# Remainders of the experts' rows in blocks of two 64-row halves, each half with its own expert's weights

## The chip, the cores and the metric

The kernel runs on one core of a Trainium2 chip. A core has five engines with queues of their own: TensorE (PE, matrix products; its weight loads are listed as PEld), VectorE (DVE), ScalarE (ACT), GpSimd (POOL) and SyncE (SP), which here does nothing but start transfers. DMA engines move data between the chip's memory and the on-chip buffers. The engines run side by side and wait for each other by semaphores; each takes its own instructions in the order in which the program lists them. The metric is the device time of one execution in microseconds (us), as the median of several runs.

## The reference

One layer of a transformer on `x` of 4 x 1024 rows by 512, in float32. The rows are normalized, then attention with 16 heads (causal mask, a bias that falls with distance) and a mixture of experts are both computed from the normalized rows, and all is added:

```
xn = layernorm(x)
out = x + attention(xn, Wq, bq, Wk, bk, Wv, bv, Wo, bo) + experts(xn, gate_w, w1, w2)

# experts: T = 4096 rows, E = 8 experts, TOP_K = 2, I = 352
probs = softmax(x @ gate_w.T)
topw, sel = top_k(probs, 2);  topw = topw / sum(topw)
g, u = split(x @ w1[e].T)                  # 512 -> 2 x 352
expert_out[e] = (silu(g) * u) @ w2[e].T    # 352 -> 512
out = sum over the two selected e of topw * expert_out[e]
```

Each row goes to two of the eight experts, so there are 8192 pairs of row and expert. How many fall to each expert is known only when the kernel runs.

## The kernel before, in words

**Routing.** After the normalization, `route()` (L479) works out on VectorE where each pair goes. The pairs are sorted by expert into blocks of 128 rows, and each expert's last block is filled up with empty rows. Eight experts can leave eight partly filled blocks, so the program has `NBLK` = 71 blocks (L76) whatever the data: (8192 - 8) // 128 + 8. `blocks` is the number of blocks of each expert, `ends` its running sum, `slot` the place of each pair, `eid` (L523) the expert of each block, and `token` (L585) the row that stands in each place. The table of `token` is made by matmuls (L539, `fill_table`) from 0/1 matrices `col`, `place` and `both`, which VectorE and ScalarE prepare. Pieces of the attention's projections (`pq`, `pk`, `pv`) are placed by hand between these steps on TensorE (L1268 to L1275).

**A block** (`expert_pieces`, L675) is computed in pieces:
- `gate(k)` (L737): first `turn_act(k - 1)` (L756), which transposes the activations of the block before (`pact`) and copies them out as `actT`, by VectorE and ScalarE; then four matmuls of 128 x 128 by 352 columns into `pgate` (L728), then tanh on ScalarE and a product on VectorE.
- `up(k)` (L748): four such matmuls into `pup`, a product on VectorE, then `load_w1(k + 1)`, then `turn(k + 1)`, which transposes the next block's rows (`pxs`, L721).
- `second_layer(k)` (L795): `down(k - 1)` (L770), three matmuls of up to 128 x 128 by 512 columns into `ye` (L776), an addition on VectorE (L785), the write of the block to `ys_d` (L786, on SyncE), `load_w2(k)`; then `load_rows(k + 3)`, a gather on GpSimd's queue.

A float32 matmul stands in the profile as two records, a transpose as one. So a block's gate is eight records, its second layer six.

**Weights.** All weights are read again for every block, because the block's expert is known only at run time: SyncE reads the expert's number from `eid` into a register (`value_load`, L681) and issues the loads with it. `w1` comes in four tiles of 352 KB (128 of the 512 input rows, gate and up together), in a ring of six buffers; `w2` in three tiles of 256, 256 and 192 KB, in a ring of four. A load into a buffer waits until the matmuls that read its former content are done. SyncE also issues the writes of `ys_d` and `o_d` and the other loads, all in program order: a transfer that waits holds those behind it.

**The order of the work.** Attention runs over 16 units (4 batches x 4 groups of four heads), in 12 steps each: `scores` (`s`), `values` (`o`), and for the next unit `largest` (`m`, the row maxima). All other pieces (the experts' pieces, the projections, the output rows) are in lists, each with a weight in us. `fill` (L1187) pops them one by one between the attention's steps, at an even rate; so the order on every engine is fixed when the program is built. The experts' pieces begin before the first unit's scores. The output rows follow the last block: `y` is the output projection, added to the two gathered expert rows.

The matmuls of `values` (L1084) use the array in strips: each of four heads has 128 x 32 weights and writes 32 partitions of the same `o`.

Of the kernel before, what the change touches and what calls it, by code (L numbers as in the profile page):

```python
# [16 lines left out]
P = 128  # L17
# [11 lines left out]
def kernel(  # L29
# [46 lines left out]
    NBLK = (T * TOP - NE) // BLK + NE  # L76
# [6 lines left out]
    eid = const.tile([P, NBLK], U32, tag="eid", name="eid")  # L83
# [29 lines left out]
    with ExitStack() as actx:  # L113
# [287 lines left out]
        def set_route():  # L401
# [13 lines left out]
            steps = ramp("steps", NB, BLK)  # L415
# [63 lines left out]
        def route():  # L479

            def prefix(src, n, name):
# [8 lines left out]

            more = after_norm("more", [P, NE, NB])
# [4 lines left out]
                ALU.is_gt,  # L496
            )
            blocks = once("blocks", [P, NE])
            nc.vector.tensor_reduce(blocks, more, mybir.AxisListType.X, ALU.add)
            ends = prefix(blocks, NE, "ends")  # L500
            first = once("first", [P, NE])
            nc.vector.tensor_tensor(first, ends, blocks, ALU.subtract)
            nc.vector.tensor_scalar(first, first, float(BLK), None, ALU.mult)
            rank = once("rank", [P, NT, NE])
            nc.vector.tensor_tensor(
                rank, p_rank, first.unsqueeze(1).to_broadcast([P, NT, NE]), ALU.add
            )
            slotf = once("slotf", [P, TOP, NT])
            for j in range(TOP):
# [3 lines left out]

            bnum = once("bnum", [P, NBLK])
            over = after_norm("over", [P, NBLK, NE])
            nc.vector.tensor_tensor(
                over,
                iota_row[:, :NBLK].unsqueeze(2).to_broadcast([P, NBLK, NE]),
                ends.unsqueeze(1).to_broadcast([P, NBLK, NE]),
# [3 lines left out]
            nc.vector.tensor_scalar(eid, bnum, float(NE - 1), None, ALU.min)  # L523
# [150 lines left out]

        def expert_pieces():  # L675
            es, w1s, w2s, rows, xsT, acts, actT = {}, {}, {}, {}, {}, {}, {}

            def load_w1(k):
                if k == NBLK:
                    return  # L680
                es[k] = nc.sync.value_load(eid[0:1, k : k + 1], min_val=0, max_val=NE - 1)  # L681
                for c in range(NC):
                    w = phase["ex"].tile([P, 2, FI], F32, tag="w1", name=f"w1_{k}_{c}", bufs=6)
                    nc.sync.dma_start(
                        w.rearrange("p g f -> p (g f)"),
                        w1r[bass.ds(es[k], 1), :, c, :].rearrange("o p f -> p (o f)"),
                    )
                    w1s[k, c] = w

            def load_w2(k):  # L690
                if k == NBLK:
# [674 lines left out]
```

## Time and profile before

| | |
|---|---|
| time, median of 3 runs | 1636.28 us (1635.67 to 1639.81) |
| the profiled execution's own time | 1648.37 us |
| its span, first to last instruction | 1646.6 us |
| mean clock granted to TensorE | 0.997 of full |
| DMA: bytes moved, mean rate | 278.94 MB, 169 GB/s |

The costliest groups of the experts' blocks, from the page (line, engine, operation, tiles and shapes, count, then busy us and mean ns of one, then idle time just before them and what ended it):

```profile
L776 PE MATMUL ye<-w,actT 128*128 128x512 f32 (+1 forms) x426 | 197.9, 600 | 2.1 <-DVE actT L765 2.1
L728 PE MATMUL pgate<-w,xsT 128*128 128x352 f32 x568 | 183.9, 464 | 1.8 <-DMA w<-in_w1T 1.4
L728 PE MATMUL pup<-w,xsT 128*128 128x352 f32 x568 | 182.4, 464 | 0.2 <-ACT pr L1038 0.2
...
w<-in_w1T SPq DMA_DIRECT2D x284, 352.0 KB
w<-in_w2T SPq DMA_DIRECT2D x142, 256.0 KB
ys_d<-yr SPq DMA_DIRECT2D x71, 256.0 KB
w<-in_w2T SPq DMA_DIRECT2D x71, 192.0 KB
```

Matmuls overlap, so the mean of one (464 ns) is longer than its share of TensorE's time: what a group costs is read from its start to the start of what follows. The three groups together are 564 us of a span of 1646.6, and TensorE waited some 4 us in front of them in all.

### The profile page before, as it was taken

What the parts mean: (1) busy time and instruction counts of PE and PEld (TensorE: products, weight loads), DVE (VectorE), ACT (ScalarE), POOL (GpSimd) and SP (SyncE); (2) the same over time, 40 slices, a digit from 0 to 9 for tenths busy, and PEclk for the clock granted to TensorE, in tenths of its full rate; (3) what the DMA queues carried; (4) which work ended last, traced back from release to release, by engine and by line L of the source; (5) the groups of instructions that cost most, each with busy time, mean ns of one, the idle gap of its engine ahead of it and who ended that gap; (6) DMA issues with size and microseconds to landing.
All of it is one profiled execution on the core that took longest, in us unless ns stands there. A gap on an engine that the chain in (4) does not pass through costs nothing.

```text
span 1646.6 us, 29019 instructions
## 1 busy us (share of the span) xinstructions
PE 1612.0 (98%) x9476; PEld 785.9 (48%) x9476; DVE 939.4 (57%) x2886; ACT 890.0 (54%) x2062; POOL 332.5 (20%) x762
## 2 busy tenths in 40 slices
PE   7999999999999999999999999999999999979999
PEld 4545545545454544545544445454444445433333
DVE  6775555655646555555555555555555555547652
ACT  5443455565656465656556474646565565646331
POOL 4610011111020102021111112010211011133660
PEclk9999999999999999999999999999999999999999
DMA  9847854547542434456452335464533424356891
GB/s 312 334 138 255 276 168 155 193 132 237 168 135 89 144 125 146 145 184 209 136 161 88 116 97 174 147 232 153 171 124 105 137 90 156 119 188 200 275 300 64
DMA packets 146486, 278.94 MB, mean 169 GB/s; under 512 B 16448, under 2 KB 45120, under 8 KB 144800
## 3 DMA queue, kind: packets, MB, share of 16 engines
q1 hardware_dynamic: 134384, 234.89, 43.3%
q0 software_dynamic: 10800, 35.40, 7.4%
q10 hardware_dynamic: 1152, 6.82, 1.0%
q8 instruction: 75, 1.23, 0.3%
q14 instruction: 75, 0.61, 0.1%
HBM read 229.07 MB, written 47.97 MB: 168 GB/s over the span
## 4 chain that ended last, share of the span: by engine, by line
PE 88%; DMA 2%; issue 1%; ACT 1%; DVE 1%; SPq 0%; another core or an unknown queue 0%; DVEq 0%; ACTq 0%
PE ye L776 11%; PE pup L728 11%; PE pgate L728 10%; PE s L1007 10%; PE o L1084 8%; PE m L893 8%; PE pk L622 6%; PE pq L622 6%; PE y L840 6%; PE pv L654 5%; PE s L1026 2%; PE pxs L721 2%; PE pact L762 2%; DMA w<-in_w1T 2%; DMA ot<-o_d 1%
## 5 line engine op out<-in xcount | busy, mean ns | idle before, releaser
L1038 ACT ACTIVATE pr<-s,kbias 128x512 f32<-128x512 f32 (+3 forms) x768 | 382.6, 581 | 387.9 <-PE s L1026 345.9
L939 ACT ACTIVATE z<-z,top 128x896 f32<-128x896 f32 (+7 forms) x512 | 391.5, 773 | 84.0 <-DVE top L929 81.0
L1046 POOL TENSOR_SCALAR_AFFINE_SELECT pr<-pr 128x128 f32<-128x128 f32 x512 | 150.4, 302 | 1105.5 <-ACT pr L1038 1099.0
L917 DVE CUSTOM_DVE_ANT_0 z<-m,rel 128x512 f32<-128x512 f32 (+3 forms) x512 | 271.5, 586 | 101.5 <-PE m L893 101.0
L776 PE MATMUL ye<-w,actT 128*128 128x512 f32 (+1 forms) x426 | 197.9, 600 | 2.1 <-DVE actT L765 2.1
L728 PE MATMUL pgate<-w,xsT 128*128 128x352 f32 x568 | 183.9, 464 | 1.8 <-DMA w<-in_w1T 1.4
L728 PE MATMUL pup<-w,xsT 128*128 128x352 f32 x568 | 182.4, 464 | 0.2 <-ACT pr L1038 0.2
L1007 PE MATMUL s<-q,k 32*128 32x512 f32 (+3 forms) x1536 | 179.4, 533 | 0.0
L893 PE MATMUL m<-k,q 32*128 32x512 f32 (+3 forms) x1536 | 172.5, 487 | 4.9 <-DVE oT L1099 4.8
L917 DVE CUSTOM_DVE_ANT_0 z<-m,rel,l 128x128 f32<-128x128 f32 (+3 forms) x256 | 125.8, 547 | 86.6 <-PE m L893 86.1
L1084 PE MATMUL o<-pr,v 128*32 128x512 f32 (+3 forms) x1536 | 144.9, 492 | 0.0
L728 PEld LDWEIGHTS pup<-w,xsT 128*128 128x128 f32 x568 | 105.6, 190 | 68.7 <-ACT pr L1038 9.9
L728 PEld LDWEIGHTS pgate<-w,xsT 128*128 128x128 f32 x568 | 101.5, 190 | 54.3 <-DMA w<-in_w1T 6.2
L622 PE MATMUL pq<-xnT,wq 128*128 128x512 f32 x256 | 119.6, 610 | 1.3 <-ACT pr L1038 0.8
L776 PEld LDWEIGHTS ye<-w,actT 128*128 128x128 f32 (+1 forms) x426 | 76.6, 190 | 90.7 <-issue 72.5
L622 PE MATMUL pk<-xnT,wk 128*128 128x512 f32 x256 | 117.8, 603 | 0.7 <-ACT pr L1038 0.7
L654 PE MATMUL pv<-wv_sb,xnT 128*128 128x512 f32 x256 | 117.0, 600 | 0.2 <-ACT pr L1038 0.2
L1007 PEld LDWEIGHTS s<-q,k 32*128 32x128 f32 x1536 | 61.1, 183 | 108.9 <-issue 82.3
L893 PEld LDWEIGHTS m<-k,q 32*128 32x128 f32 x1536 | 87.2, 185 | 45.5 <-issue 11.7
L745 DVE SCALAR_TENSOR_TENSOR th<-th,pgate 128x352 f32<-128x352 f32 x71 | 37.0, 521 | 121.7 <-ACT th L744 121.7
L939 ACT ACTIVATION_READ_ACCUMULATOR z<-z,top 128x1 f32 x512 | 100.4, 196 | 0.0
L840 PE MATMUL y<-wo_sb,ot 128*128 128x512 f32 x192 | 90.8, 622 | 6.0 <-DMA ot<-o_d 6.0
(165 smaller groups left out, 1564.1 us busy)
## 6 DMA issues: line engine op xcount, KB each, us to landing
w<-in_w1T SPq DMA_DIRECT2D x284, 352.0 KB
w<-in_w2T SPq DMA_DIRECT2D x142, 256.0 KB
ys_d<-yr SPq DMA_DIRECT2D x71, 256.0 KB
w<-in_w2T SPq DMA_DIRECT2D x71, 192.0 KB
xr<-in_x SPq DMA_DIRECT2D x32, 256.0 KB
out<-xr SPq DMA_DIRECT2D x32, 256.0 KB
xn_d<-xT ACTq DMA_DIRECT2D x6, 1024.0 KB
o_d<-oT SPq DMA_DIRECT2D x24, 256.0 KB
```

Of the source, the lines that this page charges most:

```text
L622: nc.tensor.matmul(ps, lhsT=ws[which][:, i, :], rhs=xnT[b, s][:, i, :], start=(i == 0), stop=(i == NC - 1),)
L654: nc.tensor.matmul(ps, lhsT=xnT[b, t // QT][:, i, (t % QT) * P : (t % QT + 1) * P], rhs=wv_sb[:, i, :], start=(i == 0), stop=(i == NC - 1),)
L728: nc.tensor.matmul(ps, lhsT=xsT[k][:, c, :], rhs=w1s[k, c][:, gu, :], start=(c == 0), stop=(c == NC - 1),)
L776: nc.tensor.matmul(y, lhsT=a[:m, f, :], rhs=w2s.pop((k, f))[:m, :], start=(f == 0), stop=(f == NF - 1),)
L840: nc.tensor.matmul(y, lhsT=lhsTs[c], rhs=wo_sb[:, c, :], start=(c == 0), stop=(c == NC - 1))
L893: nc.tensor.matmul(pss[h][:, col : col + n], lhsT=qs[b, c, s][r, (i % QT) * P : (i % QT + 1) * P], rhs=ks[b, c, k0 // QB][r, :n], start=Tr ...
L917: nc.vector.tensor_tensor_reduce(out=zs[h][:, z0 : z0 + n], in0=pss[h][:, col : col + n], in1=rel[:, S - L + k0 : S - L + k0 + n], scale=1 ...
L939: nc.scalar.activation(z[h][:, z0 : z0 + L], z[h][:, z0 : z0 + L], AF.Exp, bias=top[:, h : h + 1], scale=-slopes[c * HC + h], accum_out=to ...
L1007: nc.tensor.matmul(ps[:, :n], lhsT=ks[b, c, j // QT][r, (j % QT) * P : (j % QT + 1) * P], rhs=qs[b, c, s][r, q0:], start=True, stop=False,)
L1038: nc.scalar.activation(pr[:, :n], pss[h][:, :n], AF.Exp, bias=kbias[:, hh, d : d + 1], scale=-slopes[hh],)
L1046: nc.gpsimd.affine_select(out=pr[:, :P], in_=pr[:, :P], compare_op=ALU.is_ge, fill=0.0, base=0, pattern=[[1, P]], channel_multiplier=-1,)
L1084: nc.tensor.matmul(o[h * D : (h + 1) * D, q1:], lhsT=vs[b, j][:, col : col + D], rhs=prs[h][:, : QB - q1], start=(k == 0), stop=(k == len( ...
```

## The change

An expert's pairs are now split into full blocks of 128 rows and a rest. A rest takes one or two halves of 64 rows, and two halves, of whatever experts, make one mixed block. There are always at least `PURE` = 64 - 7 = 57 full blocks, numbered 0 to 56; the remaining places, up to 22 halves, make 11 mixed blocks, numbered 57 to 67. Full blocks over the 57th are computed as two halves of one expert. `NBLK` is 68. `eid` has 57 + 22 entries.

- `route()` gets more steps on VectorE: `full` and `half` counts, a second running sum, a jump `far` for rows beyond an expert's full blocks, and the experts of the halves (`overh`, `hnum`).
- A mixed block uses two experts' weights. Its matmuls go in four strips of 32 rows of the block, two with the first expert's weights and two with the second's (`strips`).
- Its `w1` comes in eight tiles of 352 KB (one expert, gate or up, two of the four chunks): six are loaded where a block's four were, the last two after its `gate`. Its second layer is computed in two halves of 256 columns, each with its own loads into the ring of `w2`: two of 256 KB and two of 96 KB.
- The mixed blocks are put between the full ones, about every sixth, the first as the fourth block. The order of the pieces differs around them: where a block or the block before it is mixed, the (first) `down` of the block before comes ahead of `up`; a mixed block's second `down` comes after it.

```diff
-    NBLK = (T * TOP - NE) // BLK + NE
+    HALF = BLK // 2
+    PURE = T * TOP // BLK - (NE - 1)
+    NBLK = PURE + (2 * (NE - 1) + NE) // 2
...
+            rows_full, over_full = small("rows_full"), small("over_full")
+            nc.vector.tensor_scalar(rows_full, full, float(BLK), None, ALU.mult)
+            nc.vector.tensor_tensor(over_full, p_count, rows_full, ALU.subtract)
+            half, half2 = small("half"), small("half2")
+            nc.vector.tensor_scalar(half, over_full, 0.0, None, ALU.is_gt)
+            nc.vector.tensor_scalar(half2, over_full, float(HALF), None, ALU.is_gt)
+            nc.vector.tensor_tensor(half, half, half2, ALU.add)
+            ends = prefix(full, NE, "ends")
+            hends = prefix(half, NE, "hends")
...
+            nc.vector.tensor_tensor(rank, p_rank, every_tile(rows_full), ALU.is_ge)
+            nc.vector.tensor_tensor(rank, rank, every_tile(far), ALU.mult)
+            nc.vector.tensor_tensor(rank, rank, every_tile(first), ALU.add)
+            nc.vector.tensor_tensor(rank, rank, p_rank, ALU.add)
...
+            blocks = list(range(PURE))
+            for n in range(NBLK - PURE):
+                blocks.insert((n + 1) * NBLK // (NBLK - PURE) - 3, PURE + n)
...
             def load_w1(k):
...
+                if mixed(k):
+                    load_two(k, 0, 0)
+                    load_two(k, 0, 2)
+                    load_two(k, 1, 0)
+                    return
...
+            def load_two(k, gu, c):
+                for i, e in enumerate(es[k]):
+                    w = w1_tile(f"{k}_{gu}_{c}_{i}")
+                    nc.sync.dma_start(
+                        w,
+                        w1r[bass.ds(e, 1), :, c : c + 2, gu * FI : (gu + 1) * FI].rearrange(
+                            "o p c f -> p (o c) f"
+                        ),
+                    )
...
+            def strips(ps, tokens, ws, **flags):
+                for q in range(P // D):
+                    cols = slice(q * D, (q + 1) * D)
+                    nc.tensor.matmul(
+                        ps[cols, :],
+                        lhsT=tokens[:, cols],
+                        rhs=ws[q * D // HALF],
+                        skip_group_check=True,
+                        **flags,
+                    )
...
             def gate(k):
-                turn_act(k - 1)
...
+                turn_act(lead.get(k))
                 ps = half_up(k, 0)
+                if mixed(k):
+                    load_two(k, 1, 2)
...
+            def down(k, part=None):
+                cols = slice(0, E) if part is None else slice(part * EH, (part + 1) * EH)
...
+                nc.vector.tensor_tensor(r[:, cols], y, bo_sb[:, cols], ALU.add)
+                if part == 0:
+                    load_w2(k, 1)
                     return
                 nc.sync.dma_start(ys_d[k * BLK : (k + 1) * BLK, :], r)
-                load_w2(k + 1)
+                load_w2(follow.get(k))
...
-            for k in range(NBLK + 1):
+            for k in blocks:
                 pieces.append((2.9, lambda k=k: gate(k)))
-                if k < NBLK:
-                    pieces.append((2.9, lambda k=k: up(k)))
-                pieces.append((2.8, lambda k=k: second_layer(k)))
+                ups = [(2.9, lambda k=k: up(k))]
+                rows_ = (0.0, lambda k=k: load_rows(ahead_of.get(k)))
+                j = lead.get(k)
+                if j is None:
+                    downs = []
+                elif mixed(j):
+                    downs = [(1.5, lambda j=j, part=part: down(j, part)) for part in range(2)]
+                else:
+                    downs = [(2.8, lambda j=j: down(j))]
+                if mixed(k) or j is not None and mixed(j):
+                    pieces += downs[:1] + ups + downs[1:]
+                else:
+                    pieces += ups + downs
+                pieces.append(rows_)
```

`follow` and `lead` are the block after and the block before in the new order, `ahead_of` the one three further on. The gathers of the rows and the final gathers from `ys_d` use the new places and are otherwise unchanged.

## The prediction

> **What bounds the kernel now.** I read the page's head and the chain of waits first, then three stretches of the span, then the timelines of TensorE, VectorE and SyncE's queue around the code that changes.
>
> ```profile
> span 1646.6 us, 29019 instructions
> PE 1612.0 (98%) x9476; PEld 785.9 (48%) x9476; DVE 939.4 (57%) x2886; ACT 890.0 (54%) x2062; POOL 332.5 (20%) x762
> PE 88%; DMA 2%; issue 1%; ACT 1%; DVE 1%; SPq 0%; another core or an unknown queue 0%; DVEq 0%; ACTq 0%
> ```
>
> TensorE is busy 98% of the span and holds 88% of the chain, so work taken from it is worth its full length, and each new TensorE wait costs its full length. The stretches (columns: busy time of PE, PEld, DVE, ACT, POOL, then clock, DMA share, GB/s):
>
> ```profile
> 78.00:106.00 28.00, 24.95 (x113) 12.59 (x112) 25.00 (x40) 12.93 (x27) 3.25 (x10) 1.00 0.03 6
> 106.00:190.00 84.00, 82.50 (x351) 45.22 (x349) 48.17 (x151) 31.41 (x83) 10.45 (x12) 1.00 0.82 274
> 190.00:1440.00 1250.00, 1246.36 (x7705) 609.29 (x7704) 696.39 (x2186) 734.25 (x1719) 184.06 (x507) 1.00 0.47 150
> ```
>
> Three different stages. From 78 to 106 us the routing tables are made and TensorE already waits for VectorE, which is busy 25.0 of 28. From 106 to 190 the first experts' blocks run almost back to back and the DMA engines are 82% full; 274 GB/s at 0.82 is 334 GB/s at full share. Afterwards attention lies between the blocks and the DMA is half empty.
>
> ```profile
> 748.78 2.53 PE L728 MATMUL pgate<-w,xsT 128*128 128x352 f32 x8
> 751.14 2.53 PE L728 MATMUL pup<-w,xsT 128*128 128x352 f32 x8
> 753.51 0.60 PE L721 MATMUL pxs<-ident,xs 128*128 128x128 f32 x4
> 754.82 2.74 PE L776 MATMUL ye<-w,actT 128*128 128x512 f32 x6
> 757.40 0.49 PE L762 MATMUL pact<-ident,act 128*128 128x128 f32 x3
> 757.73 2.53 PE L728 MATMUL pgate<-w,xsT 128*128 128x352 f32 x8
> ...
> 612.37 1.92 PE L1084 MATMUL o<-pr,v 128*32 128x512 f32 x16
> 614.23 1.14 PE L1007 MATMUL s<-q,k 32*128 32x512 f32 x8
> ```
>
> From start to next start a block costs gate 2.36, up 2.37, second layer 2.58 and pact 0.33; pxs is 0.53 (its next row, at 754.04, is left out). The attention output `o` already uses the changed blocks' form: 128 rows by 32 columns, four strips side by side. Two groups of four strips at 512 columns take 1.86 us (612.37 to 614.23).
>
> **Taken off TensorE: 3 blocks.** 3 x (2.36 + 2.37 + 0.53 + 2.58 + 0.33 = 8.17) = 24.5 us.
>
> **Strips in 11 blocks.** The `o` pair of 512 and 384 columns takes 1.64 us, 0.22 less for 128 columns: 1.66 ns a column for four strips together, and 0.15 us a run. A full-array gate run of 4 x 352 columns at the same 1.66 ns is 2.34 of its 2.36. So strips overlap fully and only the run's fixed part is new: gate and up +0.13 each, the second layer 6 x 256 x 1.66 + 2 x 0.15 = 2.85 instead of 2.58. Entering a strip run adds 0.09 to the run before (gate followed by `o` 2.46, by up 2.36), four times a block, some of which a following `o` or `s` pays already. Net 0.65 a block, 7 us in 11: TensorE's work falls by 17.5. Bounds: 20 (half the fixed part) to 12.5 (the 0.15 is paid by groups of two, not runs: 11 x 0.45 more).
>
> **Routing chain.** In order of the program the DVE's stretch from `more` to `partf` grows from 22 to 49 instructions: 3 more over 128x256, 2 over 128x352, 22 small, and two shrink from 568 to 456 columns.
>
> ```profile
> 80.66 0.17 DVE L502 TENSOR_TENSOR first<-ends,blocks 128x8 f32<-128x8 f32 x1
> 80.86 0.17 DVE L503 TENSOR_SCALAR first<-first 128x8 f32<-128x8 f32 x1
> 81.07 0.42 DVE L505 TENSOR_TENSOR rank<-routing,first 128x256 f32<-128x256 f32 x1
> 81.53 0.42 DVE L510 TENSOR_TENSOR pick<-pick,rank 128x256 f32<-128x256 f32 x1
> ...
> 89.24 1.50 PE L539 MATMUL routing<-both,place 128*128 128x142 bf16 x16 [0.37 <-DVE place L565]
> ```
>
> A small dependent one costs 0.20 to the next start, an independent one 0.07 (the copies of `ends`), a 256-wide one 0.46. 3 x 0.46 + 2 x 0.55 + 22 x 0.17 - 0.3 = 5.9, less 0.2 for the narrower `col`: 5.7 us, bounds 3.7 (all small ones at 0.07) to 6.6. Nothing hides it: the last row shows TensorE already 0.37 us too early for `place`, its three pieces of cover spent. The whole 5.7 is added.
>
> **The weights' queue.** This is what I think decides. For a mixed block k the pieces run gate(k), down(j), up(k) instead of gate, up, down (j before k, n after). SyncE issues in program order, so the loads of n's first weights, issued in up(k), are moved behind down(j)'s write of `ys_d`, which waits for TensorE and VectorE, and behind k's four loads of second-layer weights. The same queue before:
>
> ```profile
> 710.58 0.33 SPq L786 DMA_DIRECT2D ys_d<-yr  x1
> 711.11 1.52 SPq L695 DMA_DIRECT2D w<-in_w2T  x3
> 713.44 9.28 SPq L684 DMA_DIRECT2D w<-in_w1T  x4
> ...
> 752.90:755.50 2.60, 2.60 (x26) 1.72 (x25) 2.02 (x4) 2.60 (x9) 0.00 (x0) 1.00 0.87 275
> ```
>
> `ys_d` is issued 1.1 us after the second layer's modelled end (ye ended at 709.83, this issue at 710.91). Then 0.2, four loads at 0.58 each (three took 1.52), and 1.1 with the expert's register load to the end of the first w1 issue: 4.7 us after ye's end. The window is a pair of w1 tiles (704 KB) moving in 2.6 us, started 0.6 after its issue; one tile lands about 2.0 after issue, so 6.7 after ye's end. Needed: where no attention lies between, up 2.5 + pxs 0.4 + pact 0.3 - 0.16 = 3.05 later. In the changed program's order on TensorE that is so for mixed block 62; one short attention piece gives block 65 4.0 and 57 4.1; the other eight have 12 or more and pay nothing here.
> - 62: 3.6 for the first tile, then three tiles at 1.1 to 1.3 against 0.6 of matmul: +1.7. Sum 5.3.
> - 65: 4.3.
> - 57 lies in the stage with the full DMA: it moves 8 x 352 + 1408 + 512 = 4736 KB where a block moves 2624. At 334 GB/s that is 14.5 us against the 9.3 that a block takes there. Gate of the next block 5, its own gate 0.8, the one after 0.5; and down(2), now a piece (2.5 us) earlier and behind six w1 loads instead of four (1.8 us), waits 2.7. Sum 9.
> - 58 ends that stage: 1.3 at its down(7), 0.6 at its gate, 1.4 at the gate of block 9. Sum 3.3.
>
> 21.9 less 1.4 that these gates wait now: 20.5. Laying both programs' SyncE issues and TensorE runs in order at these prices gives the kernel before 1.6 us of gate waits at 300 to 330 GB/s (the page has 1.8), and between +17 and +27 for the change; those are the bounds.
>
> **Second layer sooner after pact.** With gate(k), down(j) adjacent (blocks 57, 60, 66) actT has one gate, 2.4 us, to be copied. At the end of the kernel ye came 2.35 after pact's end and had waited 2.06 of it for actT. 1.5 us in all, bounds 0 and 5.
>
> **The clock.** Waits of this length have a second price:
>
> ```profile
> 1478.00:1482.00 4.00, 0.25 (x1) 0.00 (x0) 0.21 (x1) 0.05 (x1) 1.75 (x2) 0.98 1.00 315
> 1482.00:1488.00 6.00, 5.74 (x7) 2.18 (x8) 4.15 (x11) 2.37 (x4) 1.58 (x2) 0.50 0.48 176
> ```
>
> After 4.0 us of idle TensorE ran six at clock 0.50. Three such waits (57, 62, 65): the late tiles' 1.7 hide in the slower matmuls, and about 1.3 each is left: 3.8 us, bounds 0 and 10. The routing wait's own slow period falls on a stretch that waits for VectorE anyway.
>
> The Trainium skill ("TensorE: Matmul & The Clock Gate", HAM oscillation) says only idle gaps over about 3.4 us bring the half clock. Here 2.37 us of idle before 1552.09 was followed by clock 0.57 over 1553 to 1557, so I go by the rows; by the page only block 62 would pay, and this term would be an estimated 1.3.
>
> **Sum.** -17.5 + 5.7 + 20.5 + 1.5 + 3.8 = +14.0. The profiled run took 1648.37 (span 1646.6), 12 above the median of the runs, so its successor would show 1662; the runs should give 1636.3 + 14.0 = 1650. VectorE's eleven extra adds, 11 more PSUM banks and the extra value loads lie beside TensorE's work in the half-empty stage; without that cover some 0.2 us each.
>
> **Rivals.**
> - The waits stay hidden and TensorE's saving is kept. For: DMA is 47% busy after 190 us, and eight of eleven places have attention between. Against: the order in the queue at 57, 62 and 65. If a tile lands within 3 us of ye's end only 57's byte surplus is left: -17.5 + 5.7 + 5 = -7, 1629. Faster. Chance 0.13.
> - About half the waits and no slow clock: +1, 1637. Chance 0.12, no change.
> - Every mixed block pays: its weights come in pieces of 1408 and 1024 bytes instead of 2816 and 2048, and if these halve the rate all eleven wait about 5: -17.5 + 5.7 + 55 = 1680. Against: `o` blocks and 12 us between. Chance 0.07.
> - Strips that share one weight tile don't overlap, so the diff doesn't do what it says: each pair is serial, 8 x 0.58 + 6 x 0.43 = 7.2 a block, 80 in all, 1710. Against: the four strips of `o`. Chance 0.02.
>
> **How the numbers follow.** The forecast itself, 0.66. What a measurement can tell here is about 0.3%, 4.9 us: faster 0.13, same 0.13 (0.01 of it from the forecast's low end), slower 0.74. The terms' bounds reach from about 1633 to 1664, which leaves out the faster case's lower part and the last two rivals: about 2 in 10.
>
> **What would show it.** A mixed gate run near 2.5 us with four strips at once (or 4.8: serial); the routing wait on `place` near 6; the gate after blocks 57, 62 and 65 waiting 3 us or more for w<-in_w1T, with clock 0.5 behind it; no such wait after 61, 63, 66. If those three waits are under 1 us the forecast is wrong and the kernel faster.

## The result, and the profile after

The changed kernel takes 1663.89 us, the median of 4 runs (1660.95 to 1667.27); the kernel before took 1635.97 in the same set (4 runs, 1634.70 to 1639.81). The ratio is 1.0167, with a 95% interval of 1.0139 to 1.0196: slower by 28 us. The forecast was 1650 with a range of about 1633 to 1664. The direction came out; the loss is twice the 14 us of the forecast and lies inside its range by 0.1 us, which is luck.

From the page of the changed kernel (head, chain of waits, groups with busy us, mean ns | idle time before them, and transfers with the time from issue to landing):

```profile
span 1659.0 us, 31161 instructions
PE 1604.7 (97%) x10379; PEld 762.8 (46%) x10379; DVE 937.4 (57%) x2909; ACT 888.4 (54%) x2056; POOL 330.9 (20%) x759
...
PE 91%; DMA 5%; DVE 2%; issue 1%; SPq 1%; ACT 1%; DVEq 0%; ACTq 0%
...
L867 PE MATMUL pgate<-w,xsT 128*128 128x352 f32 x456 | 155.3, 481 | 21.3 <-DMA w<-in_w1T 20.2
L918 PE MATMUL ye_None<-w,actT 128*128 128x512 f32 x342 | 161.2, 607 | 5.9 <-DMA w<-in_w2T 4.3
...
w<-in_w1T SPq DMA_DIRECT2D x316, 352.0 KB, 4.7
```

TensorE's busy time fell by 7 us, yet the span rose by 12: DMA now holds 5% of the chain where it held 2%, and the gates of the full blocks wait 20.2 us for `w1` where all gates together waited 1.4. (`ye_None` is the second layer of a full block.)

The block whose neighbour made the longest wait, mixed block 65, on TensorE (start, length, and in brackets the idle time before and who ended it):

```profile
1120.67 2.57 PE L846 MATMUL pgate<-w,xsT 128*32 128x352 f32 x32
1123.06 1.69 PE L1239 MATMUL o<-pr,v 128*32 128x512 f32 x16
...
1126.70 2.84 PE L918 MATMUL ye_None<-w,actT 128*128 128x512 f32 x6
...
1130.34 2.57 PE L846 MATMUL pup<-w,xsT 128*32 128x352 f32 x32
1132.85 0.65 PE L839 MATMUL pxs<-ident,xs 128*128 128x128 f32 x4
1133.56 0.55 PE L901 MATMUL pact<-ident,act 128*128 128x128 f32 x3
1139.72 5.03 PE L867 MATMUL pgate<-w,xsT 128*128 128x352 f32 x8 [5.61 <-DMA w<-in_w1T]
1144.68 1.12 PE L1239 MATMUL o<-pr,v 128*32 128x256 f32 x16
```

The strips cost what was forecast: 32 records of the mixed gate take 2.39 us to the next start and those of its up 2.51, so four strips do run side by side. What is slow is the gate of the next full block. SyncE's queue and, below it, VectorE's addition that `ys_d` waits for:

```profile
1130.91 0.35 SPq L930 DMA_DIRECT2D ys_d<-yr  x1
1131.46 1.00 SPq L794 DMA_DIRECT2D w<-in_w2T  x2
1132.71 0.89 SPq L805 DMA_DIRECT2D w<-in_w2T  x2
1134.41 2.07 SPq L768 DMA_DIRECT2D w<-in_w1T  x4
```

```profile
1129.52 0.55 DVE L1072 CUSTOM_DVE_ANT_0 z<-m,rel 128x384 f32<-128x384 f32 x1
...
1130.19 0.69 DVE L926 TENSOR_TENSOR yr<-ye_None,bo_sb 128x512 f32<-128x512 f32 x1
```

That is the order that the forecast named: the write of `ys_d` first, then the mixed block's four second-layer loads, then the next block's four tiles of `w1`, issued from 1134.41 on. The gate was ready to run at 1134.1 and began at 1139.72. Two things make it later than forecast: the addition came 0.65 us after ye's end (1129.54), behind one of attention's steps on VectorE (the first row above), and the first `w1` tile was of use only 5.3 us after its issue, not 2. The clock then adds to the price. Windows of the same stretch (columns: us, busy PE, PEld, DVE, ACT, POOL, granted clock, DMA share, GB/s):

```profile
1130.00:1139.00 9.00, 4.05 (x48) 1.75 (x40) 3.00 (x8) 6.10 (x19) 2.95 (x6) 0.97 0.70 218
1139.00:1146.00 7.00, 6.28 (x28) 3.16 (x32) 0.57 (x2) 0.46 (x1) 0.00 (x0) 0.55 0.38 144
1146.00:1155.00 9.00, 9.00 (x80) 3.92 (x76) 3.93 (x11) 3.71 (x7) 0.00 (x0) 1.00 0.22 71
```

The gate took 4.96 us instead of 2.4, at clock 0.55. TensorE's timeline around the first mixed block, in the stage with the full DMA, and the routing's wait:

```profile
91.93 2.00 PE L596 MATMUL routing<-both,place 128*128 128x136 bf16 x16 [5.31 <-ACT both L618]
```

```profile
148.39 4.51 PE L918 MATMUL ye_None<-w,actT 128*128 128x512 f32 x6 [2.43 <-DMA w<-in_w2T]
...
162.25 4.31 PE L867 MATMUL pgate<-w,xsT 128*128 128x352 f32 x8 [4.70 <-DMA w<-in_w1T]
166.49 1.50 PE L846 MATMUL ye<-w,actT 128*32 128x256 f32 x24
167.93 2.63 PE L867 MATMUL pup<-w,xsT 128*128 128x352 f32 x8
...
752.42 3.69 PE L867 MATMUL pgate<-w,xsT 128*128 128x352 f32 x6 [4.13 <-DMA w<-in_w1T]
```

Each of the three long runs stands behind a wait of 2.4 us or more and takes 1.7 to 1.9 times its usual length (ye 4.45 to the next start, gate 4.24). The first half of a mixed block's second layer (`ye`), 1.44 us, is again the forecast's size.

### The two profiles differ by 12 us, the medians by 28

The last stage, from the last block's second layer to the end, explains it. It begins at these rows, of the kernel before and of the changed one:

```profile
1456.19 2.81 PE L776 MATMUL ye<-w,actT 128*128 128x512 f32 x6 [2.06 <-DVE actT L765]
```

```profile
1479.96 2.81 PE L918 MATMUL ye_None<-w,actT 128*128 128x512 f32 x6 [1.08 <-DMA w<-in_w2T]
```

To the end of the span that is 190.4 us before and 179.0 after, though the change does nothing there. Up to it the changed kernel is 23.8 us behind. The first experiment found a last stage as long as the first on one chip, and the further ones shorter stages on two others; a comparison of the two profiles alone would have hidden half of the loss.

All runs in one table (us). "Middle" is from the start of the first block's gate to the start of the last second layer; "ten blocks" is the part of it up to the start of attention's first `o`, which holds the same pieces of ten blocks in every kernel (in e6 with ten records of idle matmuls among them). Idle and half clock are TensorE's in the middle, added up over the trace's matmul records and clock changes; idle leaves out the wait just ahead of the last second layer (2.06 before, 1.08 in the changed kernel). "Last" is what follows.

| kernel | median, ratio to before (95%) | first gate | middle | ten blocks | idle | half clock | last |
|---|---|---|---|---|---|---|---|
| before (profile) | 1635.97 | 112.3 | 1343.9 | 100.2 | 5.2 | 0.0 | 190.4 |
| after | 1663.89, 1.0167 (1.0139 to 1.0196) | 114.7 | 1365.3 | 116.7 | 30.4 | 20.5 | 179.0 |
| e1 before again | 1648.67, 0.9999 (0.9980 to 1.0017) | 112.4 | 1345.2 | 100.5 | 7.3 | 0.1 | 189.5 |
| e2 order only | 1841.01, one run | 113.2 | 1539.6 | 157.2 | 121.7 | 136.5 | 186.5 |
| e3 one expert | 1627.93, 0.9878 (0.9844 to 0.9912) | 117.6 | 1318.5 | 100.3 | 3.2 | 0.0 | 188.4 |
| e4 ups first | 1666.94, 1.0121 (1.0089 to 1.0154) | 115.9 | 1362.0 | 116.3 | 23.1 | 17.1 | 186.1 |
| e5 after again | 1665.22, 1.0175 (1.0157 to 1.0193) | 116.2 | 1368.1 | 119.2 | 31.3 | 30.7 | 178.7 |
| e6 kept busy | 1661.69, 1.0152 (1.0135 to 1.0169) | 115.4 | 1364.9 | 115.0 | 21.6 | 10.2 | 178.4 |
| e7 first later | 1637.81, 1.0003 (0.9993 to 1.0013) | 116.9 | 1339.4 | 98.8 | 14.0 | 10.2 | 183.1 |
| e8 later, 8 buffers | 1632.32, 0.9973 (0.9959 to 0.9987) | 117.0 | 1333.0 | 100.9 | 11.6 | 3.4 | 179.9 |
| e9 8 buffers only | 1672.49, 1.0217 (1.0197 to 1.0238) | 117.3 | 1373.6 | 119.7 | 34.3 | 30.7 | 180.2 |
| e10 as e8 | 1632.61, 0.9978 (0.9961 to 0.9994) | 117.0 | 1332.1 | 99.6 | 10.1 | 6.8 | 179.9 |
| e11 places 13, 17, ... | 1625.80, 0.9939 (0.9926 to 0.9952) | 114.9 | 1326.3 | 98.9 | 8.6 | 3.4 | 179.9 |
| e12 places 17, 21, ... | 1628.73, 0.9943 (0.9929 to 0.9957) | 116.1 | 1329.9 | 100.6 | 11.7 | 3.6 | 182.0 |

e1 to e4 ran on one chip, where the kernel before took 1649.09; e5 to e8 on a second (1636.35); e9 to e12 on a third (1636.81).

The column of the ten blocks shows something that the single waits hide. In the changed kernel's places two of these blocks are mixed ones (57 and 58); with the later places none is. The stretch grows from 100.2 us to 116.7 (119.2 in e5). The rest of the middle, where the three blocks are saved, grows by 4.9 us (5.2 in e5), while e3, without the second expert's weights, has it 25.5 shorter. Against e3 the changed kernel thus loses 16.4 us at two mixed blocks in the ten and 30.4 at the nine others. The ten blocks are the stage with the full DMA: 26.4 MB at 263 GB/s before, 29.8 MB at 255 GB/s after. At the rate before, the 3.4 MB more are an estimated 13 us of the 16.5.

### The profile page after: what moved, and what is told of

The parts are those of the page before. It is cut to its first block, busy times and chain, and to the rows that moved or that the text cites. A ratio compares the mean times of both kernels' runs of the same rounds, so it can differ in the third digit from the quotient of the medians.

```text
span 1659.0 us, 31161 instructions
## 1 busy us (share of the span) xinstructions
PE 1604.7 (97%) x10379; PEld 762.8 (46%) x10379; DVE 937.4 (57%) x2909; ACT 888.4 (54%) x2056; POOL 330.9 (20%) x759
## 4 chain that ended last, share of the span: by engine, by line
PE 91%; DMA 5%; DVE 2%; issue 1%; SPq 1%; ACT 1%; DVEq 0%; ACTq 0%
PE s L1162 10%; PE ye_None L918 9%; PE pup L867 8%; PE pgate L867 8%; PE m L1048 8%; PE o L1239 8%; PE pk L679 7%; PE pq L679 7%; PE pv L711 6%; PE y L995 6%; DMA w<-in_w1T 2%; PE s L1181 2%; PE pxs L839 2%; PE ye L846 2%; PE pup L846 1%; PE pact L901 1%
## 5 line engine op out<-in xcount | busy, mean ns | idle before, releaser
L867 PE MATMUL pgate<-w,xsT 128*128 128x352 f32 x456 | 155.3, 481 | 21.3 <-DMA w<-in_w1T 20.2
L918 PE MATMUL ye_None<-w,actT 128*128 128x512 f32 x342 | 161.2, 607 | 5.9 <-DMA w<-in_w2T 4.3
L867 PE MATMUL pup<-w,xsT 128*128 128x352 f32 x456 | 147.9, 467 | 0.0
L711 PE MATMUL pv<-wv_sb,xnT 128*128 128x512 f32 x256 | 117.0, 600 | 0.0
L867 PEld LDWEIGHTS pgate<-w,xsT 128*128 128x128 f32 x456 | 82.7, 195 | 70.0 <-DMA w<-in_w1T 18.5
L867 PEld LDWEIGHTS pup<-w,xsT 128*128 128x128 f32 x456 | 83.5, 190 | 58.3 <-ACT pr L1193 12.8
L1094 ACT ACTIVATION_READ_ACCUMULATOR z<-z,top 128x1 f32 x512 | 100.9, 197 | 0.0
L918 PEld LDWEIGHTS ye_None<-w,actT 128*128 128x128 f32 x342 | 61.2, 192 | 79.5 <-issue 57.7
```

The costliest lines, as they stand in the source:

```text
L711: nc.tensor.matmul(ps, lhsT=xnT[b, t // QT][:, i, (t % QT) * P : (t % QT + 1) * P], rhs=wv_sb[:, i, :], start=(i == 0), stop=(i == NC - 1),)
L867: nc.tensor.matmul(ps, lhsT=xsT[k][:, c, :], rhs=w1s[k, c][:, gu, :], start=(c == 0), stop=(c == NC - 1),)
L918: nc.tensor.matmul(y, lhsT=a[:m, f, :], rhs=w2s.pop((k, f))[:m, :], **flags)
L1094: nc.scalar.activation(z[h][:, z0 : z0 + L], z[h][:, z0 : z0 + L], AF.Exp, bias=top[:, h : h + 1], scale=-slopes[c * HC + h], accum_out=to ...
```

## The experiments

The theory: the changed order of the pieces puts the next block's `w1` behind `ys_d` and the mixed block's second-layer weights in SyncE's queue, and TensorE waits at a few gates and then runs at half clock. The rivals: the second expert's bytes make the waits; the buffers are too few; the order is harmless and the strips or the routing cost more than forecast.

**e1, the kernel before again.** No edit.

> The kernel before, unchanged, for a second profile. The changed kernel's profile is 12.4 us longer than the kernel before's, but the medians differ by 28. Up to the 85th values run (84 in the count from 0) the changed kernel is 24 us behind, and regains 12 in the last stage. Theory: the kernel before's first profile was held up in its last stage by 12 us (TensorE idle 4.0 us, then clock 0.5), which its other executions don't have; expected: a span of about 1635 and no gap over 2.5 us after 1458 us. Rival: the profiler makes this kernel longer whenever it is on; then the span is 1647 again.

The kernel took 1648.67 against 1649.09 of its twin on that chip, with a last stage of 189.5 us; the expected 1635 failed. On this chip both medians of the kernel are near 1649, on the two others they are 1636 to 1637, so the 1648.37 of the profile before need not be an exception of one execution; on which chip it was taken isn't on record. All four kernels profiled on this chip have a last stage of 186.1 to 189.5, and all eight on the other two have 178.4 to 183.1. What makes the last stage longer there stays open (each of the three chips was used for one group of runs, so the chip and the hour can't be told apart); since ratios are taken within one set, they are free of it.

**e2, the order alone.** The kernel before, with no mixed block and no strips, but at every block the order that the change has around mixed ones:

```diff
                 pieces.append((2.9, lambda k=k: gate(k)))
+                pieces.append((2.8, lambda k=k: second_layer(k)))
                 if k < NBLK:
                     pieces.append((2.9, lambda k=k: up(k)))
-                pieces.append((2.8, lambda k=k: second_layer(k)))
```

> The kernel before with one thing of the change alone: at every one of the 71 blocks the pieces run gate(k), down(k-1), up(k), so that the next block's w1 loads stand behind ys_d and the w2 loads in SyncE's queue. No strips, no mixed blocks, the old routing. Theory (the queue's order makes the waits): 3.5 to 4.5 us of gate wait at each of the first 8 blocks and at some 22 later places without attention between, none elsewhere; +120 to +150 us, more with the slow clock behind each wait: 1755 to 1800. Rival (the doubled bytes make the waits, not the order): no bytes are added, so within 1% of 1636.

It took 1841.01, 192 us more, beyond what the theory gave. The waits of TensorE (us in total, times, longest):

```profile
PE pgate L728 <- DMA w<-in_w1T: 98.7, 49, 5.4
```

Not one byte or instruction is added here. 49 gates wait up to 5.4 us, the length seen at blocks 57, 62 and 65, and 136.5 us of the middle run at half clock. The order by itself is enough for such waits; the rival in which it is harmless is out. How much of the changed kernel's own loss it makes is another question, for e3, e4 and e7.

**e3, mixed blocks with one expert's weights.** The strips, the 68 blocks and the longer routing stay; the second expert's weights are left out, so mixed blocks load what full ones do, and the order is the old one:

```diff
-                            [w1s.pop((k, gu, c, i)) for i in range(2)],
+                            [w1s[k, c][:, gu, :]] * 2,
...
-                if mixed(k) or j is not None and mixed(j):
-                    pieces += downs[:1] + ups + downs[1:]
-                else:
-                    pieces += ups + downs
+                pieces += ups + downs
```

> The change with the second expert's weights left out: a mixed block loads its first half's expert as a full block does, uses it in all four strips, and runs in the old order of pieces (rows of the second halves get the wrong expert). Strips, two-part second layer, 68 blocks and the new routing stay. Theory: TensorE -17.5 and routing +5.7, waits as before: 1636 - 12 = 1624, 1620 to 1629. Rival (strips or routing are what costs): 1650 or more.

1627.93, ratio 0.9878: 21 us faster than before on its chip, more than the 12 that were expected. With the typical length of every kind of TensorE run (the median of its kind with the same follower) added up, the middle's work is 1303.9 us against 1321.4 of the kernel before: 17.5 less, the forecast's number for 3 blocks less the strips. The number leans on how kinds are told apart: with shapes and the number of records kept apart too it is 16.0. The rest of the middle's gain, 8 us, is 3 us of idle time (4.3 against 7.3, the wait ahead of the last second layer counted in) and lengthened runs that aren't resolved. The price of the routing is in it too: 5.2 us of wait at the routing's matmuls. So all of the loss comes with the second expert's weights and their order, that of the first ten blocks too: they take 100.3 us here, as in the kernel before.

**e4, ups ahead again at the mixed blocks.** Only the blocks that follow a mixed one keep the new order:

```diff
-                if mixed(k) or j is not None and mixed(j):
+                if j is not None and mixed(j):
```

> The change with a mixed block's own order of pieces put back: gate(k), up(k), down(j); the block after it keeps the split second layer. The next block's w1 loads stand ahead of ys_d and w2 again. Theory: the gate waits behind 57, 62 and 65 (4.7, 4.1 and 5.6 us) fall under 1, down(2) no longer waits 2.4; but the last two up tiles, loaded only after half the gate, lose the cover of down: up waits of 4 us at 57, 3 at 58 and 65. Waits 8 us less in all, 1652 to 1660. Rival (the bytes alone): 1664 as the change, with waits at the same gates.

1666.94, ratio 1.0121. TensorE's waits:

```profile
PE pgate L867 <- DMA w<-in_w1T: 8.0, 6, 2.1
...
PE pup L846 <- DMA w<-in_w1T: 7.2, 12, 2.0
```

The gates behind the mixed blocks wait 8.0 instead of 20.2 us, as the theory wants, but now the mixed blocks' own ups wait 7.2, because their last two tiles are loaded only after the gate has freed a buffer. So the order in the change buys time for these two tiles and pays for it at the next gate. Idle time falls by 7 us in all: a part of the loss, not its whole. The first ten blocks hardly gain (116.3 us against 116.7 and 119.2): there the order around the mixed blocks isn't what holds TensorE up.

**e5, the changed kernel again,** beside e6 and e7. No edit.

> The changed kernel, unchanged, beside the kernel before on the same chip as the next three. The kernel before took 1636 in one set of runs and 1649 in another, with the same work up to the last block, so the ratio is what counts. Theory: the loss lies before the last block and does not depend on the chip: 1.013 to 1.020 again, with waits of 3 us or more at the gates behind mixed blocks 57, 62 and 65. Rival (the loss came from that chip's memory): 1.000 to 1.010.

1665.22, ratio 1.0175, the same as the first time within the interval. The waits are at the same gates (5.7 us in two parts at 161 to 167, 4.18 at 757.7, 5.14 at 1145.0); the half clock lasts 30.7 us instead of 20.5, at the same places and one more (179.3). Against the profile before, the first gate is 3.9 us later and the middle 24.2 longer, together 28.1, which is what the medians say (28.9).

**e6, TensorE kept busy in the three waits.** The changed kernel with matmuls that nobody reads, of 128x128 by 512 columns, ahead of the gates behind blocks 57, 62 and 65:

```diff
                 turn_act(lead.get(k))
+                spare = {57: 5, 62: 4, 65: 5}.get(lead.get(k), 0)
+                if spare:
+                    idle = bank([P, E], F32, name=f"idle_{k}")
+                    for _ in range(spare):
+                        nc.tensor.matmul(idle, lhsT=ident, rhs=wo_sb[:, 0, :], start=True, stop=True)
```

> The changed kernel with 5, 4 and 5 matmuls more, of 128x512, whose result nobody reads, in front of the gates behind 57, 62 and 65: TensorE works 4.3, 3.4 and 4.3 us where it waited 4.7, 4.1 and 5.6. Theory (the slow clock is a price of its own behind a wait): the half-clock windows at these three gates, 13.7 us long together, go; the gates run at full speed or wait for their later tiles; 2 to 6 us faster than the change although TensorE does 12 us more. Rival (behind the wait the gates are held by their tiles anyway): within 1 us of the change, or slower.

1661.69 against 1665.22: 3.5 us faster although 14 matmuls of 0.89 us (12 us) were added. The two ratios' intervals overlap, so the time alone doesn't settle it; the rows say more. Behind block 65, first in e5 and then in e6:

```profile
1136.12 2.57 PE L846 MATMUL pup<-w,xsT 128*32 128x352 f32 x32
...
1145.03 4.57 PE L867 MATMUL pgate<-w,xsT 128*128 128x352 f32 x8 [5.14 <-DMA w<-in_w1T]
1149.53 0.86 PE L1239 MATMUL o<-pr,v 128*32 128x256 f32 x16
```

```profile
1132.14 2.57 PE L846 MATMUL pup<-w,xsT 128*32 128x352 f32 x32
...
1135.74 4.46 PE L882 MATMUL idle<-wo_sb,ident 128*128 128x512 f32 x10
1140.88 1.66 PE L867 MATMUL pgate<-w,xsT 128*128 128x352 f32 x4 [0.68 <-DMA w<-in_w1T]
1143.27 1.72 PE L867 MATMUL pgate<-w,xsT 128*128 128x352 f32 x4 [0.73 <-DMA w<-in_w1T]
1144.92 0.86 PE L1244 MATMUL o<-pr,v 128*32 128x256 f32 x16
```

From the up to the `o` behind the gate it is 13.41 us without and 12.78 with the useless work. With it the gate runs at full speed (clock 1.00 from 1136 to 1144) and waits for its later tiles instead: most of what the clock gives back, the weights take. Over the middle the half clock falls from 30.7 to 10.2 us. Over the three places, from the up of the mixed block to what follows the gate behind it, e6 takes 4.3 us less than e5 and 3.1 less than the first profile of the changed kernel. So the slow clock is a price of its own, and about 3 to 4 us of it were had back without touching the queue.

**e7, the old order at the mixed blocks and later places.** As e4, and the mixed blocks stand at places 12, 17, 22 and so on, so that the stage with the full DMA holds none:

```diff
-                blocks.insert((n + 1) * NBLK // (NBLK - PURE) - 3, PURE + n)
+                blocks.insert(12+5*n, PURE + n)
```

> The change with two edits: a mixed block keeps gate, up, down, and the mixed blocks stand at places 12, 17, ... 62 of the 68, none in the stage where the DMA engines are 80% full. Theory: the wait behind 57 and its neighbours (some 20 us with the slow clock) goes, and no w1 load stands behind ys_d and w2; left are 2 to 3 us at two places where no attention lies between gate and up, and the routing's 5.3. So near the kernel with one expert's weights (ratio 0.988), 4 to 8 us above it: 0.990 to 0.994 of the kernel before, faster than both. Rival (twice the weights cost wherever the blocks stand): 1.008 or more.

1637.81, ratio 1.0003: 27 us better than the changed kernel, no better than the kernel before, so the expectation of 0.990 to 0.994 failed. Against e4 (1.0121) only the places differ: that is 19 us, and the ten blocks, now all full ones, take 98.8 us. The later places alone, with the order of the change, were not run. TensorE still waits in the middle for 14.0 us; a new wait is that of the mixed blocks' second layers:

```profile
PE ye L846 <- DMA w<-in_w2T: 5.2, 3, 2.8
```

**e8, the same with eight `w1` buffers.** All eight tiles of a mixed block are loaded at one time; the activations are written over the tanh tile, and one table lies with the routing's, to make room:

```diff
-                return phase["ex"].tile([P, 2, FI], F32, tag="w1", name=f"w1_{name}", bufs=6)
+                return phase["ex"].tile([P, 2, FI], F32, tag="w1", name=f"w1_{name}", bufs=8)
...
                     load_two(k, 1, 0)
+                    load_two(k, 1, 2)
...
-                if mixed(k):
-                    load_two(k, 1, 2)
...
-                acts[k] = phase["ex"].tile([P, FI], F32, tag="act", name=f"act_{k}", bufs=2)
-                nc.vector.scalar_tensor_tensor(acts[k], th, 0.5, ps, ALU.mult, ALU.mult)
+                nc.vector.scalar_tensor_tensor(th, th, 0.5, ps, ALU.mult, ALU.mult)
```

> As the one before, with a ring of eight w1 buffers instead of six, so that all eight tiles of a mixed block are loaded when its turn comes and none after its gate (room: the activations are written over the tanh, one early constant is freed with the routing's buffers). Theory: the up waits of the last pair go, some 3 us better than with six: 0.988 to 0.993. Rival (loads issued together share the DMA engines, so that the first of eight lands later than the first of six): no better than with six, gate waits instead of up waits.

1632.32, ratio 0.9973, the interval wholly below 1: faster than both kernels, though not by as much as expected (0.988 to 0.993). Idle 11.6, half clock 3.4.

**e9, eight buffers alone,** in the changed kernel's order and places.

> The changed kernel, its order of the pieces and its places for the mixed blocks kept, with a ring of eight w1 buffers in place of six, so that all eight tiles of a mixed block are loaded together behind the block before it (the activations are written over the tanh tile and one table lies with the routing's, to make room). Theory (the order in SyncE's queue makes the waits, not a lack of buffers): no faster than the changed kernel, ratio to the kernel before 1.015 or more, TensorE's idle time between the first gate and the last second layer 30 us or more; the waits move from the gates to the second layers, because two more w1 issues now stand ahead of the second-layer weights. Rival (buffers were missing): ratio 1.003 or less, idle time under 12 us, because all loads may start earlier.

1672.49, ratio 1.0217, idle 34.3: slower than the change itself. TensorE's waits:

```profile
PE pgate L868 <- DMA w<-in_w1T: 20.1, 12, 4.7
PE ye_None L916 <- DMA w<-in_w2T: 9.4, 4, 3.3
```

The gates wait as long as with six buffers (20.2), and the second layers 9.4 instead of 4.3, since two more issues stand ahead of their weights. A lack of buffers is out as the cause of the loss in this order; the buffers help only in the order of e8, where a mixed block's up follows its gate at once.

**e10, e11, e12, other places.** e10 is e8 again; e11 and e12 move the mixed blocks:

```diff
-                blocks.insert(12+5*n, PURE + n)
+                blocks.insert(13+4*n, PURE + n)
```

> The version with the old order around the mixed blocks, eight w1 buffers and the mixed blocks at places 12, 17, 22 and so on, once more, as the measure for the next two. Expected: the ratio of the first time, 0.9973, within 0.002; span near 1630 if the last stage takes its 178 us.

> The same version with the mixed blocks at places 13, 17, 21 and so on (every fourth block instead of every fifth). Theory: what keeps the version of the line above from its full saving is a few waits whose place follows from which attention pieces lie beside a mixed block; laying the two programs' SyncE issues and TensorE runs in order at 300 to 330 GB/s gives 1.4 to 3.1 us less wait here, so the ratio to the kernel before is 0.001 to 0.002 lower: 0.9955, and the 3.4 us wait for second-layer weights near 1028 us is gone. Rival: the places hardly matter after block 12, same ratio within 0.001. Either way not below 0.9925: the saving of 17.5 less the routing's 5 is 12.5 us of 1636.

> As the line above, with the first mixed block at place 17 in place of 13 (17, 21, 25 and so on). Theory: by the same working 1.4 to 3.3 us less wait than with places 12, 17, 22, so 0.9955 as well; the first mixed block lies further from the full DMA of the first blocks, which is worth nothing if place 12 was late enough already. Rival (the first stage still pays at place 12 and 13): 0.002 lower than the line above.

e10 repeats its ratio (0.9978). e11 has 0.9939 and e12 0.9943: 11 us below the kernel before in e11 and 7 below e10, more than the 1.4 to 3.1 us of waits that the expectation counted. TensorE's waits of e10 and then of e11:

```profile
PE ye L847 <- DMA w<-in_w2T: 3.3, 1, 3.3
PE pgate L868 <- DMA w<-in_w1T: 2.7, 5, 0.9
```

```profile
span 1621.2 us, 31124 instructions
...
PE pgate L868 <- DMA w<-in_w1T: 3.8, 2, 3.0
```

The second-layer wait of 3.3 us is gone, as expected, and the half clock behind it. Of the 7 us, idle time is 1.5 and half clock some 1.7 (3.4 us at half speed); 2.1 is an earlier first gate, which the places don't touch and which differs by 1.5 between two profiles of one kernel (after and e5). The rest isn't resolved. The rival of e12, that the first stage still pays at place 13, is out: later is no better.

**What they say together.** Ratios are compared here across chips, and each step stands on the one before it, so the parts could come out differently in another order. The changed kernel (1.0167 and 1.0175) and e3 (0.9878) lie 47 to 49 us apart. The old order at the mixed blocks is worth some 8 us of that (1.0121), the later places 19 (1.0003), eight buffers 4 to 5 (0.9973 and 0.9978), other places 6 (0.9939), and 10 us are still left. So the order in the queue is enough to make such waits, but it is not the largest part here: that is the places of the mixed blocks (from e4 to e7 the ten blocks alone go from 116.3 to 98.8 us). That it costs so much because the second expert's bytes meet DMA engines that are already 80% busy fits the estimate of 13 us, but isn't isolated; the old order with eight buffers at the first places was not run. The rival "the second expert's bytes make the waits" therefore holds in part.

## Why the prediction was right, and where its sizes were off

- **Three blocks less and strips in eleven, -17.5.** About right: -17.5 (or -16.0) by the typical lengths of e3, and the strip runs at 2.39 to 2.51 us for a gate or up and 1.43 to 1.44 for half a second layer. The rival of serial strips (4.8 us) is out by the first row of the timeline.
- **Routing, +5.7.** Nearly right. The wait on the routing's matmuls is 5.31 us, near the 6 that was said to show it. The first gate is only 2.4 us later than before (3.9 in e5), but that is counted from the start of the span, and the routing's chain itself began earlier in this execution: VectorE's `more` starts at 78.55 before and at 76.30 after, and between 76.3 and 78.7 in the profiles with the new routing. The chain's end is at these rows, before and after:

```profile
85.33 0.23 DVE L531 CAST partf<-part 128x128 f32<-128x128 uint32 x1
```

```profile
88.06 0.23 DVE L588 CAST partf<-part 128x128 f32<-128x128 uint32 x1
```

  From `more` to `partf` that is 6.8 us before and 11.8 after: 5.0 more. From the same start to the first gate it is 4.6 more (5.7 in e5). The second wait that the kernel before had in this chain is under 0.3 us in the changed kernel, whose later routing matmuls find their tables ready or nearly so, and gives a part back:

```profile
97.40 1.19 PE L539 MATMUL routing<-both,place 128*128 128x142 bf16 x16 [2.16 <-DVE both L572]
```

- **The waits behind SyncE's queue, +20.5, and the second layer's +1.5.** The places are right: 57 and its neighbours, 58 with the gate after it, 62 and 65. In this profile no gate after 250 us but those behind 62 and 65 has an idle stretch above 0.6 us, so none behind 61, 63 or 66. Both of the forecast's mechanisms are there: the order in the queue (e2 shows that it makes such waits by itself) and, at 57 and 58, the full DMA (in e4 the ten blocks stay as long, in e3 and e7 they don't). e9 shows that buffers don't cure the waits. The idle time in the middle, the wait ahead of the last second layer counted in, rose from 7.3 to 31.5, by 24.2 (25.0 in e5), against the forecast's 22.0.
- **What was too short there: the landing of the first tile.** The working took 2.0 us from issue, read from a pair of tiles moving alone in a quiet stretch. Behind the second-layer weights and `ys_d`, with three more tiles issued right after it, the first tile was of use 5.3 us after its issue at block 65; the page gives 4.7 as the median of all. The three gates with a long wait stood 4.70, 4.13 and 5.61 us, where the gate behind 57 was counted at 5 and the first tile of the two others at 3.6 and 2.6. The late tiles, counted at 1.7 each, then cost 0.41 at one gate and nothing at the other two, whose gates ran at half speed. So the waits of these gates add up to 14.9 us where the forecast had 5 + 5.3 + 4.3 = 14.6, because two errors cancelled. That transfers in flight together share the engines is the likely reason (DMA share 0.70 in that window); no run here isolates it.
- **The clock, +3.8 with bounds 0 and 10.** This term was the most wrong. The middle is 21.4 longer: -17.5 of work and 24.2 of idle leave 14.7 (16.7 in e5). TensorE worked through 19.1 of the 20.5 us at half clock, and half of that, 9.6, is an estimate of what the clock took; in e5 it is 11.9 (23.8 of 30.7). About 5 us are left in both and aren't resolved. The step that was too small is "the late tiles' 1.7 hide in the slower matmuls, and about 1.3 each is left" at three places. In the changed kernel there are five stretches of half clock in the middle, two of them behind waits of 2.06 and 2.43 us that the step didn't count.
- **The skill's rule and the row.** The Trainium skill ("TensorE: Matmul & The Clock Gate", HAM oscillation) gives about 3.4 us of idle time as the least that brings the half clock. Here half clock came behind 2.06 us (at 249.8) and 2.43 (at 148.4), while another 2.06 us (at 177.3) had none; where the page and these rows differ, the rows decide. By the rule three places would have paid; the rows give five. Going by the row was right and still not enough.
- **The sum.** +14.0 forecast; e5, whose profile agrees with the medians, shows 28.1. The difference is an earlier start of the routing's chain in e5 (-1.8, nothing of the change; the routing itself took its 5.7), the idle time (25.0 for 22.0, +3.0) and the clock with what goes beside it (16.7 for 3.8, +12.9). The rivals with fewer waits (1629, 1637) are out. So is the one in which every mixed block pays 5 us at a gate: where attention lies between, no gate after 255 us waits more than 0.8 in either profile. That the second expert's bytes cost nothing there isn't shown: with all mixed blocks in the half-empty stage e7 still takes 20 us more than e3.
- **The profiled run.** The forecast put the successor of the profile at 1662, 12 us above its median. It was 1660.95, but for another reason: its last stage was 11 us shorter, and the loss up to there larger. Two errors of about the same size cancelled in the profile; the medians show the loss.

## What to carry to other kernels

When a piece is moved, write down the order of issues in the queue that feeds it, and count from the last thing that this queue waits for to the first tile's landing as measured in a crowded stretch, not a quiet one. Add the clock: a wait of 2 us or more on TensorE may run the next 3 to 7 us at half speed; here 24.2 us of waits took about 9.6 more in that way. Mind where pieces that load more stand: two mixed blocks in a stage whose DMA engines are already 80% busy lost 16.4 us against e3, the nine others 30.4. Work saved on the bound engine (17.5 us here) is kept only with an order, places and buffers that let the weights arrive: the same change with the old order, eight buffers and the mixed blocks at places 13, 17, 21 and so on takes 1625.80 us, 0.9939 (0.9926 to 0.9952) of the kernel before.

## What was not expected of the hardware

- Half clock comes in stretches of 3.4 or 6.8 us (once 10.2, in e2). In every profile here they begin whole multiples of 3.41 us apart. They can follow as little as 1.05 us of idle time, but not each time: ahead of the last second layer e11 waited 1.05 us and ran on at half clock, while the changed kernel waited 1.08 and ran on at full speed (2.81 us, shown above).

```profile
1441.21 4.51 PE L916 MATMUL ye_None<-w,actT 128*128 128x512 f32 x6 [1.05 <-DMA w<-in_w2T]
```

- The same kernel took 1649 us on one chip and 1636 to 1637 on two others. In the profiled kernels the last stage, output projection with gathers and writes, is where they differ (186.1 to 189.5 us against 178.4 to 183.1); its cause wasn't tried.
- Over the whole changed kernel a 352 KB tile took 4.7 us (median) from issue to landing, and 5.3 the first one behind block 65, against about 2, worked out from a pair in a quiet stretch of the kernel before.
